# The last eight GRU cells: products gate by gate in three banks, another form of the new state, idle products behind a step's products

## The chip, the cores and the metric

The kernel runs as one program on one core of a Trainium2 chip. The metric is the device time of one launch in microseconds (us). Three runs of the kernel before took 2911.01, 2905.47 and 2907.79 us; the median is 2907.79 us. The profile and the trace are of one further execution, which took 2913.18 us; its first and last instruction are 2911.3 us apart.

The engines are named as the profile names them: PE multiplies matrices (PEld is its weight load), DVE, ACT and POOL are the vector, scalar and general engines, and SP issues the DMAs. All arithmetic is in float32.

## The reference, cut to what matters

Four layers follow each other, each added to the running x of shape 8 x 256 x 512: a masked attention, an attention with modulation, a network of 512 coupled oscillators that is stepped over the 256 columns with a fourth-order Runge-Kutta rule, and a GRU that is stepped over the same 256 columns. The change touches only the end of the last one:

```
def cell(h, x):
    gi = x @ W_ih + b_ih
    gh = h @ W_hh + b_hh
    i_r, i_z, i_n = jnp.split(gi, 3, axis=-1)
    h_r, h_z, h_n = jnp.split(gh, 3, axis=-1)
    r = jax.nn.sigmoid(i_r + h_r)
    z = jax.nn.sigmoid(i_z + h_z)
    n = jnp.tanh(i_n + r * h_n)
    h_new = (1.0 - z) * n + z * h
    return (h_new, h_new)
```

The batch is 8 and h has 512 features. GRU step tau needs the oscillators' output of step tau (its x) and the GRU's state of step tau - 1.

## The kernel before, in words

`scans` runs the oscillators and the GRU side by side. The loop variable t counts oscillator steps; the GRU runs `LAG` = 7 steps behind, at tau = t - 7. So the loop goes on for 8 more rounds, t = 256 to 263, in which `osc` is false and only the GRU works: the cells 248 to 255 and the products of the steps 249 to 255. These eight rounds are called the tail here. The order of the work is written out by hand (`tc.manual_schedule()`): each engine does its instructions in the order in which the loop emits them.

A GRU step has two parts. `gru_products(tau, s)` (L791) multiplies the state by the recurrent weights: 4 blocks k of the contraction times 3 gates times 4 output blocks j, 48 products in all, spread over the sub-steps s = 1, 2, 3 by `FILL` (8, 20 and 20 products). Each shows as two matmul instructions in the trace, so a step has 96. The three gates share one PSUM tile `pg_ps`: the state tile `hzs[tau % 3]` holds the state at three offsets among zeros, so that gate g of a block lands in rows 8g to 8g+7 of each group of 32 rows.

The cell comes in four pieces. `gru_1` (L808) transposes the whole tile (L810), adds the input part of all three gates at once (L812), takes the tanh for r (L817) and z (L819) on ACT, and forms z, z h and 1 - z on POOL (L821, L823, L825). `gru_2` forms n's argument on DVE (L829, L831) and its tanh on ACT (L832). `gru_3` multiplies n by 1 - z (L835). `gru_4` adds z h and writes the new state three times (L840, 96 columns), and POOL adds it to the output tile `x3T` (L847).

The rest of the tail: `input_gates(c, part)` (L771) multiplies x by the input weights for the next group of `TS` = 4 steps, at t = 256, 257 and 258, ahead of the step's recurrent products. `input_gate_out` (L782) transposes one gate of that (L784) and adds its bias on POOL (L786); there are three, two at t = 258 and one at t = 259. `write_out(c)` (L849) transposes 4 finished steps (L852) and issues 4 DMAs on SP (L854). `keep_warm(rounds)` (L859) issues products whose result nobody reads, 4 a round, into `idle_ps`. In the tail it runs at s = 3 of every round, between the products of s = 2 and those of s = 3 (L893), and at s = 0 where there is no input product (L891).

`ic_ps` are the two PSUM tiles of the oscillators' coupling products (L760, read by L952). Nothing uses them after t = 255.

Of the kernel before, what the change touches and what calls it, by code (L numbers as in the profile page):

```python
# [8 lines left out]
F32 = mybir.dt.float32  # L9
AF = mybir.ActivationFunctionType  # L10
ALU = mybir.AluOpType
# [3 lines left out]
P = 128  # L15
B, T, D = 8, 256, 512
# [574 lines left out]
def scans(ctx, tc, cst, bias, b_ih, b_hh, x2T, out):  # L591
# [51 lines left out]
    def rows(j):  # L643
        return slice(32 * j, 32 * j + 32)
# [156 lines left out]
                    )  # L801

    gru = {}

    def of_step(tau):
        return slice(B * (tau % TS), B * (tau % TS) + B)

    def gru_1(tau):  # L808

        nc.vector.transpose(pgt.rearrange("p m n -> p (m n)"), pg_ps)  # L810
        v = tmp.tile([P, 12, B], F32, tag="v", name=f"v_{tau}", bufs=2)
        nc.vector.tensor_add(  # L812
            v.rearrange("p (g m) b -> p g m b", m=NJ),
            pgt.rearrange("p m (g b) -> p g m b", b=B)[:, 0:3],
            gis[tau // TS % 3].rearrange("p (g m) n -> p g m n", m=NJ)[:, 0:3, :, of_step(tau)],
        )
        nc.scalar.activation(tr, v[:, 0:4, :], AF.Tanh, scale=0.5)  # L817
        tz = tmp.tile([P, NJ, B], F32, tag="tz", name=f"tz_{tau}", bufs=2)
        nc.scalar.activation(tz, v[:, 4:8, :], AF.Tanh, scale=0.5)  # L819
        z = tmp.tile([P, NJ, B], F32, tag="z", name=f"z_{tau}", bufs=2)  # L820
        nc.gpsimd.tensor_scalar(z, tz, 0.5, 0.5, ALU.mult, ALU.add)  # L821
        zh = tmp.tile([P, NJ, B], F32, tag="zh", name=f"zh_{tau}", bufs=2)
        nc.gpsimd.tensor_tensor(zh, z, hzs[tau % 3][:, :, 0:B], ALU.mult)  # L823
        z1 = tmp.tile([P, NJ, B], F32, tag="z1", name=f"z1_{tau}", bufs=2)
        nc.gpsimd.tensor_scalar(z1, tz, -0.5, 0.5, ALU.mult, ALU.add)  # L825
        gru.update(v=v, zh=zh, z1=z1)

    def gru_2(tau):
        stt(nn1, tr, 1.0, gru["v"][:, 8:12, :], ALU.add, ALU.mult)  # L829
        nn = tmp.tile([P, NJ, B], F32, tag="nn", name=f"nn_{tau}", bufs=2)  # L830
        stt(nn, nn1, 0.5, gis[tau // TS % 3][:, 12:16, of_step(tau)], ALU.mult, ALU.add)  # L831
        nc.scalar.activation(tn, nn, AF.Tanh)  # L832

    def gru_3():
        nc.vector.tensor_mul(hm, tn, gru["z1"])  # L835

    def gru_4(tau):

        hz = hzs[(tau + 1) % 3]
        nc.vector.tensor_tensor(  # L840
            state3(hz),
            hm.unsqueeze(2).to_broadcast([P, NJ, 3, B]),
            gru["zh"].unsqueeze(2).to_broadcast([P, NJ, 3, B]),
            ALU.add,
        )
        x = x3T[tau // TS][:, :, of_step(tau)]
        nc.gpsimd.tensor_tensor(x, x, hz[:, :, 0:B], ALU.add)  # L847

    def write_out(c):  # L849

        o = two.tile([P, NJ, 32], F32, tag="o", name=f"o_{c}")
        nc.vector.transpose(o.rearrange("p m n -> p (m n)"), x3T[c].rearrange("p m n -> p (m n)"))  # L852
        for j in range(NJ):
            nc.sync.dma_start(  # L854
                out[:, c * TS : (c + 1) * TS, j * P : (j + 1) * P].rearrange("b t n -> t b n"),
                o[rows(j)].rearrange("p m n -> p (m n)"),
            )

    def keep_warm(rounds):  # L859

        for k in range(rounds):
            for j in range(NJ):
                nc.tensor.matmul(
                    idle_ps[32 * j : 32 * j + B, :],
                    lhsT=condS[:, k, :],
                    rhs=cT_sb[:, k, j * P : (j + 1) * P],
                    start=True,
                    stop=True,
                )

    with tc.manual_schedule():
        made = []
        for t in range(T + LAG + 1):
            osc = t < T
            tau = t - LAG
            prod, cell = 0 <= tau < T, 1 <= tau <= T
            inp = TS <= t < T + TS
            c, part = t // TS - 1, t % TS
            if osc:
                if t % TS == 0:  # L880
                    x3T[t // TS] = chp.tile([P, NJ, 32], F32, tag="x3T", name=f"x3T_{t // TS}")
                qs = q
            for s in range(4):
                n = f"{t}_{s}"
                ic = ic_ps[s % 2]

                if osc:
                    coupling(tT, ic)
                if inp and s == 0:
                    input_gates(c, part)  # L890
                if t < T + LAG and (not prod or s == 0) and not (inp and s == 0 and INPUTS[part]):  # L891
                    keep_warm(2)
                if not osc and t < T + LAG and s == 3:  # L893
                    keep_warm(2)

                if osc:
                    sq, mm, hq = sqmm[:, 0, s % 2], sqmm[:, 1, s % 2], hqs[:, s % 2]
                    nc.scalar.activation(sq, qs, AF.Square, scale=math.sqrt(CUB[s]))  # L898
                if cell and s == 0:
                    gru_1(tau - 1)  # L900
                if cell and s == 1:
                    gru_2(tau - 1)

                if osc:
                    if s == 3:
                        stt(W[:, 4], qs, PQ[3], W[:, 4], ALU.mult, ALU.add)
                        p = st.tile([P, NJ, B], F32, tag="p", name=f"p_{t}")
                        nc.vector.tensor_scalar(p, W[:, 4], CLAMP - OFF, -CLAMP - OFF, ALU.min, ALU.max)  # L908
                    stt(mm, sq, LIN[s], qs, ALU.subtract, ALU.mult)  # L909
                if cell and s == 1:  # L910
                    gru_3()
                if osc:
                    nc.vector.tensor_sub(hq, W[:, s], mm)  # L913
                if cell and s == 1:
                    gru_4(tau - 1)
                if prod:
                    gru_products(tau, s)
                if osc:
                    if s < 3:
                        take(s, qs)  # L920
                    if s == 2 and t // US_CH + 1 < T // US_CH:
                        drive(t // US_CH + 1, t % US_CH // NJ, t % NJ)
                    if t == 0 and s < 3:

                        for i in range(*((0, 5), (5, 10), (10, 16))[s]):
                            drive(0, i // NJ, i % NJ)
                    if 0 < t < TS and s > 0:
                        gru_init(3 * t - 3 + s - 1)
                    if t == TS and s == 1:
                        gru_init(9)  # L930
                    if s == 3 and t + 1 < T:
                        W_next = linear_p(t + 1, p)

                if s == 3:

                    now, made = made, []
                    if cell and (tau - 1) % TS == TS - 1:
                        made.append((tau - 1) // TS)
                    if not osc:
                        now, made = now + made, []  # L940
                    for x in now:
                        write_out(x)
                if inp and (part, s) in ((2, 2), (2, 3), (3, 2)):
                    input_gate_out(c, {(2, 2): 0, (2, 3): 1, (3, 2): 2}[part, s])

                if osc:
                    qn = tmp.tile([P, NJ, B], F32, tag="qn", name=f"qn_{n}", bufs=4)
                    tTn = []
                    for half in range(2):
                        m2 = slice(half * HM, (half + 1) * HM)  # L950
                        icT = tmp.tile([P, HM, 32], F32, tag=f"icT{half}", name=f"icT{half}_{n}", bufs=2)
                        nc.vector.transpose(icT.rearrange("p m n -> p (m n)"), ic[:, half * 64 : half * 64 + 64])  # L952
                        stt(qn[:, m2, :], icT[:, :, 0:B], IC[s], hq[:, m2, :], ALU.mult, ALU.add)  # L953
                        if s < 3 or t + 1 < T:

                            tTn.append(tanh_half(qn, half, n))
                    tT = tTn
                    qs = qn
            if osc:
                q = st.tile([P, NJ, B], F32, tag="q", name=f"q_{t}")  # L960
                nc.gpsimd.tensor_scalar(q, qs, CLAMP, -CLAMP, ALU.min, ALU.max)
                if t + 1 < T:
                    W = W_next
                x = x3T[t // TS][:, :, of_step(t)]
                nc.gpsimd.tensor_tensor(x, x2T[:, :, :, t], q, ALU.add)  # L965
# [98 lines left out]
```

## Time and profile before

| what | us |
|---|---|
| median of three runs (lowest, highest) | 2907.79 (2905.47, 2911.01) |
| the profiled execution | 2913.18 |
| its span | 2911.3 |
| last oscillator transpose on DVE ends | 2857.6 |
| first product of GRU steps 249, 250, 251, 252 starts | 2860.51, 2866.25, 2871.99, 2877.72 |
| first product of GRU steps 253, 254, 255 starts | 2885.12, 2890.86, 2898.26 |
| last transpose of the output (L852) starts | 2905.99 |

The tail is thus some 53 us of the 2911.3 us. In it, one cell waits for one step's products and the next step's products wait for that cell. The table gives the start of each step's first product, so that the difference of two neighbours is a step. Before the tail the oscillators set the pace and the GRU's work lies between theirs.

### The profile page before, as it was taken

The page shows a single profiled execution, that of the slowest core. Times are in us where ns is not written, and L with a number is a line of the kernel's source. Part 1 is how long each engine was busy: PE and PEld are TensorE (multiplying, and loading weights), DVE is VectorE, ACT ScalarE, POOL GpSimd, SP SyncE. Part 2 cuts the span into 40 slices and gives each one's busy share as a digit, 9 for nine tenths or more (in the row PEclk, how much of TensorE's full clock was granted, in tenths as well). Part 3 has the DMA queues.
Part 4 walks back from the last instruction along what each step waited for, and adds up shares of the span by engine and source line. Part 5 has one row for each costly group of instructions (what it writes and reads, how often), then busy time and mean ns, then how long its engine had stood idle before and what let it go on. Part 6 is the DMA issues. An engine that isn't in the chain of part 4 may idle for free.

```text
span 2911.3 us, 159789 instructions
## 1 busy us (share of the span) xinstructions
PE 2711.6 (93%) x67258; PEld 1922.8 (66%) x67258; DVE 2127.1 (73%) x8951; ACT 1719.3 (59%) x8427; POOL 1096.2 (38%) x2945
## 2 busy tenths in 40 slices
PE   8799999999989999999999999999999999999996
PEld 3244444444557777777777777777777777777776
DVE  6767777775357777777777777777777777777773
ACT  5666566664346666666666666666666666666651
POOL 0134333443213444444444444444444444434442
PEclk7899999999999999999999999999999999999999
DMA  3111110101600000000000000000000000000000
GB/s 145 40 41 41 37 41 26 48 19 34 130 2 5 7 6 7 6 7 6 7 6 7 7 6 7 7 6 6 8 6 7 6 7 6 7 7 6 6 7 6
DMA packets 27559, 57.58 MB, mean 20 GB/s; under 512 B 2817, under 2 KB 17165, under 8 KB 24789
## 3 DMA queue, kind: packets, MB, share of 16 engines
q1 hardware_dynamic: 26836, 47.36, 5.3%
q8 instruction: 525, 8.60, 1.2%
q14 instruction: 198, 1.61, 0.2%
HBM read 40.15 MB, written 7.21 MB: 16 GB/s over the span
## 4 chain that ended last, share of the span: by engine, by line
PE 57%; DVE 28%; ACT 8%; issue 4%; POOL 1%; DMA 1%; ACTq 0%; SPq 0%; POOLq 0%; DVEq 0%
PE pg L795 20%; PE ic L760 18%; DVE icT L952 5%; DVE qn L953 5%; PE psqkv L321 5%; ACT tT L660 4%; DVE hqs L913 3%; PE pc L254 3%; DVE own L810 3%; DVE sqmm L909 2%; DVE v L812 2%; PE pc L167 2%; PE s L211 2%; DVE hz L840 2%; PE n L372 1%
## 5 line engine op out<-in xcount | busy, mean ns | idle before, releaser
L760 PE MATMUL ic<-cT_sb,tT 128*8 128x128 f32 x32736 | 1086.5, 273 | 81.3 <-ACT tT L660 44.5
L760 PEld LDWEIGHTS ic<-cT_sb,tT 128*8 128x8 f32 x32736 | 760.0, 89 | 338.5 <-ACT tT L660 267.9
L795 PE MATMUL pg<-whh_sb,hz 128*32 128x128 f32 x24576 | 821.2, 275 | 49.8 <-DVE hz L840 17.8
L660 ACT ACTIVATE tT<-qn 128x16 f32<-128x16 f32 x2046 | 441.0, 216 | 637.6 <-DVE qn L953 516.8
L795 PEld LDWEIGHTS pg<-whh_sb,hz 128*32 128x32 f32 x24576 | 670.3, 110 | 124.0 <-DVE hz L840 123.2
L952 DVE STREAM_TRANSPOSE icT<-ic 128x64 f32<-128x64 f32 x2048 | 504.6, 246 | 66.8 <-PE ic L760 62.2
L953 DVE SCALAR_TENSOR_TENSOR qn<-icT,hqs 128x16 f32<-128x16 f32 x2048 | 350.7, 171 | 70.1
L755 POOL TENSOR_TENSOR W<-W,cx 128x128 f32<-128x128 f32 x765 | 297.4, 389 | 256.3 <-ACT cx L741 256.2
L748 POOL TENSOR_TENSOR W<-cx,us 128x128 f32<-128x128 f32 x255 | 116.9, 458 | 444.5 <-ACT cx L741 444.5
L909 DVE SCALAR_TENSOR_TENSOR sqmm<-sqmm,qn 128x32 f32<-128x32 f32 x768 | 153.6, 200 | 151.9 <-ACT sqmm L898 122.7
L913 DVE TENSOR_TENSOR hqs<-W,sqmm 128x32 f32<-128x32 f32 x1020 | 200.1, 196 | 46.4 <-DVE own L835 1.3
L774 PE MATMUL gi<-wih_sb,x3T 128*32 128x384 f32 (+2 forms) x3072 | 201.5, 379 | 0.5 <-POOL x3T L965 0.5
L741 ACT ACTIVATE cx<-qn 128x32 f32<-128x32 f32 x1280 | 200.9, 213 | 0.0
L321 PE MATMUL psqkv<-wqkv_sb,xnT 128*128 128x512 f32 x384 | 174.6, 600 | 2.9 <-ACT sc L216 2.7
L221 DVE TENSOR_REDUCE mxp<-sc 128x4 f32<-128x2048 f32 x64 | 146.1, 2283 | 38.0 <-ACT sc L216 38.0
L741 ACT ACTIVATE cx<-p 128x32 f32<-128x32 f32 x1020 | 149.8, 217 | 32.1 <-DVE p L908 1.3
L216 ACT COPY sc<-s 128x512 f32<-128x512 f32 x256 | 131.8, 609 | 45.6 <-PE s L211 45.6
L239 DVE TENSOR_TENSOR sc<-sc,bc 128x2048 f32<-128x2048 f32 x64 | 148.5, 2321 | 9.6 <-DMA bc<-row 9.5
L810 DVE STREAM_TRANSPOSE own<-pg 128x128 f32<-128x128 f32 x256 | 84.8, 331 | 94.6 <-PE pg L795 94.6
L243 ACT ACTIVATE sc<-sc,negT 128x2048 f32<-128x2048 f32 x64 | 129.1, 2020 | 35.8 <-DVE sc L239 35.8
L741 ACT ACTIVATE cx<-q 128x32 f32<-128x32 f32 x1020 | 145.5, 213 | 0.0
L898 ACT ACTIVATE sqmm<-qn 128x32 f32<-128x32 f32 x768 | 140.5, 183 | 0.8
(149 smaller groups left out, 3360.4 us busy)
## 6 DMA issues: line engine op xcount, KB each, us to landing
bc<-row SPq DMA_DIRECT2D x16, 1024.0 KB
x<-in_x SPq DMA_DIRECT2D x8, 512.0 KB
out<-o SPq DMA_DIRECT2D x256, 16.0 KB
wqkv_sb<-in_L_cond_W_qkv SPq DMA_DIRECT2D x1, 3072.0 KB
wih_sb<-in_L_cond_W_ih SPq DMA_DIRECT2D x4, 768.0 KB
whh_sb<-in_L_cond_W_hh SPq DMA_DIRECT2D x4, 768.0 KB
x2d<-x2o SPq DMA_DIRECT2D x11, 256.0 KB
x2T<-x2d SPq DMA_DIRECT2D x11, 256.0 KB
```

What stands on the lines that cost most here:

```text
L321: nc.tensor.matmul(ps, lhsT=xnTs[b][:, c, m * P : (m + 1) * P], rhs=wqkv_sb[:, c, part * D : (part + 1) * D], start=(c == 0), stop=(c == N ...
L660: nc.scalar.activation(tT, src[:, half * HM : (half + 1) * HM, :], AF.Tanh)
L741: nc.scalar.activation(c[:, i], x, AF.Copy, scale=f)
L755: nc.gpsimd.tensor_tensor(W[:, i + 1 : 5], W[:, i + 1 : 5], c, ALU.add)
L760: nc.tensor.matmul(ps[32 * j : 32 * j + B, :], lhsT=tT[k // HM][:, k % HM, :], rhs=cT_sb[:, k, j * P : (j + 1) * P], start=(k == 0), stop= ...
L774: nc.tensor.matmul(gi_ps[rows(j), g0:g1, :], lhsT=x3T[c][:, k, :], rhs=wih_sb[:, k, g0:g1, j * P : (j + 1) * P], start=(k == 0), stop=(k = ...
L795: nc.tensor.matmul(pg_ps[rows(j), :], lhsT=hzs[tau % 3][:, k, 32 * g : 32 * g + 32], rhs=whh_sb[:, k, g, j * P : (j + 1) * P], start=((k, ...
L810: nc.vector.transpose(pgt.rearrange("p m n -> p (m n)"), pg_ps)
L909: stt(mm, sq, LIN[s], qs, ALU.subtract, ALU.mult)
L913: nc.vector.tensor_sub(hq, W[:, s], mm)
L952: nc.vector.transpose(icT.rearrange("p m n -> p (m n)"), ic[:, half * 64 : half * 64 + 64])
L953: stt(qn[:, m2, :], icT[:, :, 0:B], IC[s], hq[:, m2, :], ALU.mult, ALU.add)
```

## The change

For t < 256 the emitted order is as before. For t >= 256 the loop body is a branch of its own. Cell 248 still uses `gru_1` to `gru_4`; the cells 249 to 255 use `tail_cell`, and the products of the steps 249 to 255 come from `tail_products`.

`tail_products` runs the gates one after the other in the order r, n, z (g = 0, 2, 1), each over all four blocks k, each into a PSUM tile of its own: `pg_ps` and the two `ic_ps`. `tail_sum` transposes one gate and adds its input part. `tail_cell` does r, then n, then z, and forms the new state as n + z (h - n): with tz = tanh(z's argument / 2), that is 0.5 (tz + 1) (h - n) + n, on DVE. The new state is written once, not three times.

In a round the cell now comes first, then (at t = 259) all three `input_gate_out`, the step's products, the input products, the idle products (2 rounds behind input products, else 6, none in the last two rounds) and the output.

```
+    gate_ps = (pg_ps, *ic_ps)
...
+    def tail_products(tau):
+        for g in (0, 2, 1):
+            for k in range(NJ):
+                for j in range(NJ):
+                    nc.tensor.matmul(
+                        gate_ps[g][rows(j), :],
+                        lhsT=hzs[tau % 3][:, k, 0:32],
+                        rhs=whh_sb[:, k, g, j * P : (j + 1) * P],
+                        start=(k == 0),
+                        stop=(k == NJ - 1),
+                    )
+
+    def tail_sum(tau, g):
+        x = tmp.tile([P, NJ, 32], F32, tag="tg", name=f"tg_{tau}_{g}", bufs=2)
+        nc.vector.transpose(x.rearrange("p m n -> p (m n)"), gate_ps[g])
+        v = tmp.tile([P, NJ, B], F32, tag="tv", name=f"tv_{tau}_{g}", bufs=4)
+        gi = gis[tau // TS % 3][:, 4 * g : 4 * g + 4, of_step(tau)]
+        nc.vector.tensor_add(v, x[:, :, 0:B], gi)
+        return v
+
+    def tail_cell(tau):
+
+        h, hz = hzs[tau % 3][:, :, 0:B], hzs[(tau + 1) % 3]
+        vr = tail_sum(tau, 0)
+        nc.scalar.activation(tr, vr, AF.Tanh, scale=0.5)
+        vn = tail_sum(tau, 2)
+        stt(nn1, tr, 1.0, vn, ALU.add, ALU.mult)
+        nn = tmp.tile([P, NJ, B], F32, tag="nn", name=f"nn_{tau}", bufs=2)
+        stt(nn, nn1, 0.5, gis[tau // TS % 3][:, 12:16, of_step(tau)], ALU.mult, ALU.add)
+        nc.scalar.activation(tn, nn, AF.Tanh)
+        vz = tail_sum(tau, 1)
+        tz = tmp.tile([P, NJ, B], F32, tag="tz", name=f"tz_{tau}", bufs=2)
+        nc.scalar.activation(tz, vz, AF.Tanh, scale=0.5)
+        d = tmp.tile([P, NJ, B], F32, tag="zh", name=f"d_{tau}", bufs=2)
+        nc.vector.tensor_sub(d, h, tn)
+        e = tmp.tile([P, NJ, B], F32, tag="z", name=f"e_{tau}", bufs=2)
+        stt(e, tz, 1.0, d, ALU.add, ALU.mult)
+        stt(hz[:, :, 0:B], e, 0.5, tn, ALU.mult, ALU.add)
+        x = x3T[tau // TS][:, :, of_step(tau)]
+        nc.gpsimd.tensor_tensor(x, x, hz[:, :, 0:B], ALU.add)
...
-                    lhsT=condS[:, k, :],
-                    rhs=cT_sb[:, k, j * P : (j + 1) * P],
+                    lhsT=condS[:, k % NJ, :],
+                    rhs=cT_sb[:, k % NJ, j * P : (j + 1) * P],
...
+            if not osc:
+                if cell and tau - 1 >= T - LAG:
+                    tail_cell(tau - 1)
+                elif cell:
+                    gru_1(tau - 1)
+                    gru_2(tau - 1)
+                    gru_3()
+                    gru_4(tau - 1)
+                if inp and part == 3:
+                    for g in range(3):
+                        input_gate_out(c, g)
+                if prod:
+                    tail_products(tau)
+                if inp:
+                    input_gates(c, part)
+                if prod and t + 1 < T + LAG:
+                    keep_warm(2 if inp and INPUTS[part] else 6)
+                if cell and (tau - 1) % TS == TS - 1:
+                    made.append((tau - 1) // TS)
+                for x in made:
+                    write_out(x)
+                made = []
+                continue
...
-                    keep_warm(2)
-                if not osc and t < T + LAG and s == 3:
                     keep_warm(2)
...
-                    if not osc:
-                        now, made = now + made, []
```

## The prediction

> **What bounds the kernel now.** Nothing before the last oscillator step is edited, so I looked for the stretch that can move. The page first: PE is busy 93% of the span, but that is an average over three layers and says nothing of a tail of 53 us. Then the chain of waits in the tail, GRU step 253 from its first product to that of step 254 (columns: start, length, what; "x56" counts matmul instructions):
>
> ```profile
> 2885.12 1.74 PE pg L795 x56
> 2886.86 0.44 PE idle L863 x16
> 2887.30 1.14 PE pg L795 x40
> ...
> 2888.46 0.34 DVE own L810
> ...
> 2888.82 0.27 DVE v L812
> ...
> 2889.25 0.22 ACT tz L819
> ...
> 2889.55 0.23 POOL z L821
> ...
> 2889.85 0.25 POOL zh L823
> 2890.10 0.19 POOL z L825
> ...
> 2890.32 0.21 DVE own L835
> ...
> 2890.55 0.27 DVE hz L840
> ...
> 2890.86 2.63 PE pg L795 x56
> ```
>
> The reader is to see a ring with no slack: products 3.34 us (2885.12 to 2888.46), then the cell 2.40 us (to 2890.86), 5.74 us together. Sixteen idle instructions stand inside the products and cost 0.44. The cell's bound is z's way over POOL, not n's.
>
> Some steps are longer: 7.40 us for 252 and 254, and step 255 too. The table of stretches says why (length, then busy time of PE, PEld, DVE, ACT and POOL, then the granted clock); I cut it every 3.41 us, the spacing on which the slow stretches fall:
>
> ```profile
> 2864.10:2867.51 3.41, 1.80 (x60) 1.32 (x56) 1.18 (x6) 0.55 (x3) 0.90 (x4) 1.00 0.02 5
> ...
> 2887.99:2891.40 3.41, 1.37 (x52) 1.08 (x47) 1.44 (x6) 0.55 (x3) 0.90 (x4) 1.00 0.04 7
> 2891.40:2894.81 3.41, 3.41 (x76) 3.25 (x72) 0.00 (x0) 0.00 (x0) 0.00 (x0) 0.52 0.00 0
> 2894.81:2898.23 3.42, 1.42 (x48) 1.13 (x40) 1.44 (x6) 0.55 (x3) 0.65 (x3) 0.98 0.02 5
> 2898.23:2901.64 3.41, 3.38 (x65) 3.27 (x69) 0.00 (x0) 0.00 (x0) 0.25 (x1) 0.52 0.00 0
> ```
>
> A stretch in which PE was busy 1.37 or 1.42 us is followed by one at clock 0.52; after 1.80 it is not. There are three such cold stretches (the first at 2877.75), each adding 7.40 - 5.74 = 1.66 us.
>
> **The change, part by part.**
>
> *Products.* A step keeps its 96 instructions. The idle ones leave the middle: -0.44. Pace: 40 instructions take 1.09 us from start to start (2887.01 to 2888.10 on the weight load), 27.3 ns each; 112 of them then make 3.06, and DVE started at 3.34, so 0.28 is the pipeline and the release. Counted from the step's first product, r's 32 are readable at 0.87 + 0.28 = 1.15, n's at 2.03, z's at 2.90.
>
> Can DVE read one bank while PE fills another? The timeline of the last oscillator step shows it:
>
> ```profile
> 2856.77 1.28 PE L795 MATMUL pg<-whh_sb,hz 128*32 128x128 f32 x40
> 2857.02 0.25 DVE L952 STREAM_TRANSPOSE icT<-ic 128x64 f32<-128x64 f32 x1 [0.26 <-PE ic L760]
> 2857.30 0.17 DVE L953 SCALAR_TENSOR_TENSOR qn<-icT,hqs 128x16 f32<-128x16 f32 x1
> 2857.39 0.24 DVE L952 STREAM_TRANSPOSE icT<-ic 128x64 f32<-128x64 f32 x1
> ```
>
> The transpose of `ic` starts under the products into `pg`. And the second transpose, which needs nothing of L953, starts 0.09 after it, while L953, which needs its transpose, started 0.28 after that one: independent DVE instructions overlap.
>
> *The cell.* Durations: a 128x128 transpose from PSUM to SBUF 0.30 (L784 in the tail), next dependent start 0.33; a 128x32 add or three-operand instruction 0.19 to 0.20 (L829, L831, L835), next start 0.23; tanh to its DVE reader 0.23 (2889.11 to 2889.34). r: transpose 1.15, add 1.48, tanh 1.71, usable 1.94. n: transpose 2.03, add 2.36, L829's kind 2.59, L831's kind 2.82, tanh 3.05, usable 3.28. z: ready at 2.90, but DVE is in order, so behind 2.82 by some 0.1: transpose 2.93, add 3.26, tanh 3.49, usable 3.72. h - n goes beside z's tanh (3.38 to 3.58). Then e 3.72, the new state 3.95, and PE starts 0.25 later (L840's 0.31 with 258 ns; 96 columns become 32, 200 ns): **4.20 us a step**. So 1.54 less than 5.74: 0.44 of idle products and 1.10 of the cell (2.40 to 1.30 behind the last product). If DVE lets nothing overlap, z starts at 3.05 and the step is 4.32; I take 4.20, since the row above shows overlap, and keep 4.32 for the range.
>
> Here a rule speaks against the change. The Trainium skill, "VectorE: DVE Perf Modes", section on the TRN2 errata, says that latency is paid per instruction, so that many small tiles cost more than one large. DVE goes from 6 to 11 instructions a cell, and with all of them in the ring a step is 5.75 (worked out under the second rival). The rows put r's and n's six under the products, with only z's behind them: 4.20. I take the rows.
>
> *Idle products and clock.* They now stand behind the products: 48 instructions (6 rounds), 1.31 us, so PE has issued everything at 2.62 + 1.31 = 3.93, before the state is there at 4.20: no cost, 0.27 of slack. PE is then busy over 90% of a step, and cold stretches should go. Behind input products it is 0.87 + 0.44 of the same.
>
> One gap opens instead. Before, the input products of t = 256 ran while cell 248 was computed (16 instructions, 1.07 us). Now step 249's products stand ahead of them, so PE waits from 2858.05 (last product of 248) to 2860.51 (state there): 2.46 us. The Trainium skill, "TensorE: Matmul & The Clock Gate", section "Why this matters for your kernels", says that gaps above about 3 us between bursts throttle. By that, 2.46 is free, but so were the 2.04 us gaps that went cold here. By the rows it is a stretch from 2857.27 to 2860.68 with about 1 us busy, below the 1.42 that went cold: 3.41 us at half clock, +1.66. I take the row. The 3.41 us grid is not tied to the kernel: on a random phase a gap g goes cold if about 1.8 of it falls into one stretch, 67% for 2.46 (28% with no boundary inside, 39% with one near an end), 54% for 2.04.
>
> *Moved work.* At t = 259 three gate transposes and the one of `write_out` follow cell 251 on DVE, ahead of step 252's r. The third waits for a buffer (two of them) until POOL has added the first gate (0.25 for `x3T`, then 0.46 each): DVE is free at about 1.35, r's transpose slips by 0.20, and r's tanh has 2.59 - 1.94 = 0.65 to spare: nothing. Without that cover it is 0.2 once. The four DMAs of that chunk go to an SP queue that has nothing else; POOL loses three instructions a cell; its last addition of gates ends near 1.6, before or just at the add that might ask for it (1.48).
>
> *The end.* For cell 255 the state comes at 3.95, POOL's addition 4.23, L852 4.52. What follows (5.3 us to the end of the span) stays.
>
> **Sum.** Before, 2860.51 to 2905.99 is 45.48. After: 6 x 4.20 + 4.52 = 29.72, less by 15.8: 10.8 of work and 5.0 of three cold stretches. With +1.66 for the new gap it is -14.1: the profiled execution's 2913.18 would be 2899.1. The median of the runs is 5.4 lower; some of that can be fewer cold stretches. With four gaps of 2.04 at 54%, a run has 2.2 of them, 3.6 us. So against the median: 10.8 + 3.6 - 0.67 x 1.66 = 13.3, and **2894.5**.
>
> **The rivals.**
>
> *The clock stays as it was* (11%): idle products behind the last real one don't hold it, and three cold stretches stay beside the new gap's. 2907.79 - 10.8 + (3 - 2.2) x 1.66 + 1.1 = 2899.4. For: idle products inside the step did not prevent 1.4 of 3.41. Against: those covered 0.6 us of a gap of 2 to 2.7, the new ones nearly all.
>
> *It doesn't do what it says* (8%, and 2% for other ways to no change): DVE gets r's bank only when all products are done, or r's release comes late. Then DVE's instructions stand in line from 2.90: r's transpose 2.90 and add 3.23, n's transpose 3.46, add 3.79, L829's kind 4.02, L831's kind 4.25, z's transpose 4.48, add 4.81, tanh 5.04, e 5.27, state 5.50, PE 5.75. The tail is 6 x 5.75 + 6.07 = 40.6, plus 1.1 for the new gap, against 44.2 (45.48 with 2.2 cold stretches in place of 3): 2905.3, no change. The `ic` row speaks against it.
>
> *Slower* (5%): the idle products become the bound. PE takes its instructions in order, so the next step's products wait for 48 idle ones. At half clock these take 2.62, far above the slack; a step is then 144 x 54.6 ns = 7.86, the last 5.24 + 1.90 = 7.14, the tail 54.3 against 44.2: 2917.9. It decides from about four of seven steps cold ((44.2 - 29.7) / 3.66). Against: the fully busy stretches in the table are followed by clock 0.98 or 1.00, so a cold stretch should heal after 3.41 us.
>
> **The numbers.** 74% for the forecast, 11, 8 + 2 and 5% for the others. About 0.2% (5.8 us) is what a measurement here can tell from no change. Faster: 74 + 11 = 85%; same 10%; slower 5%. Range: low, all cold stretches gone and none new, from a median that had three (10.8 + 5.0 = 15.8, 2892.0), less 3 for the scatter of three runs (5.5 wide); high, the first rival's 2899.4 with 0.8 for DVE without overlap and 1.3 of scatter. So 2889 to 2901.5.
>
> **What would show it.** Right: first products of the steps 250 to 255 come 4.2 us apart; r's and n's transposes start under the products; e and the state follow z's tanh, POOL is out of the ring; clock 0.5 once at most, at the start of the tail. Wrong: r's transpose starts behind z's last product; PE starts a step at the end of its idle products and not on the state; clock 0.5 in later steps; or the stretch before 2857 differs, where no edit reaches.

## The result and the profile after

Six runs of the changed kernel took 2889.26 to 2902.27 us, median 2894.74; the kernel before, with three further runs, has a median of 2908.74. The ratio is 0.9954, with a 95% interval of 0.9941 to 0.9967: 9.6 to 17.2 us less. The forecast was 2894.5.

The profiled execution of the changed kernel is the fastest of the six: 2889.26 us, span 2887.5, so 23.8 us less than the span before. Not all of that is the change. Step 249's first product starts at 2851.02 in place of 2860.51, so 9.5 us of it lie ahead of the tail, where nothing was edited. The view of one line's instructions (count, shortest, median and longest ns, first and last start) shows where, by the oscillators' first tanh; before, then after:

```profile
L660 ACT ACTIVATE tT<-qn x2046: 197/216/221, 837.6 to 2856.0; 128x16 f32<-128x16 f32 x186
```

```profile
L660 ACT ACTIVATE tT<-qn x2046: 199/216/218, 828.1 to 2846.5; 128x16 f32<-128x16 f32 x186
```

The 9.5 us are there at the first of the 2046 instructions and unchanged at the last: they arise ahead of it, where the two attention layers are. The traces' records of the clock go with that. Ahead of this tanh they show half clock for 85.3 us before and for 61.4 us after; over the fourteen profiles it is 61 to 79 us in the eight whose oscillators start by 833.6 us, and 82 to 92 us in the six where they start at 837.4 or later. Why one execution has more of it than another was not tested.

So I read every kernel below on its tail, from the first product of step 249 to the start of the last output transpose. One profile gives that to some 0.1 us where no stretch is at half clock, since the same step repeats to 0.02 us from profile to profile. The table of stretches for the tail (length, busy time of PE, PEld, DVE, ACT, POOL with the number of instructions, granted clock; the last two columns, on DMA, are not used here), before and after:

```profile
2860.51:2905.99 45.48, 31.32 (x880) 28.13 (x880) 11.20 (x48) 3.85 (x21) 7.83 (x32) 0.89 0.02 5
```

```profile
2851.02:2882.18 31.16, 27.62 (x912) 24.47 (x912) 17.13 (x83) 4.42 (x21) 3.30 (x11) 1.00 0.03 8
```

45.48 became 31.16, and the clock 0.89 became 1.00: 14.3 us, of which 5.0 are the three cold stretches and 9.3 is work that left the ring. The 5.3 us behind the last transpose are the same. DVE's busy time went up, from 11.20 us in 48 instructions to 17.13 in 83, as the objection in the prediction had it, but most of that lies under the products. The chain of waits for one step of the changed kernel (an instruction is listed from where it takes over, so one that overlaps its predecessor starts later here than in a timeline):

```profile
2868.68 1.08 PE pg L856 x32
2869.77 0.92 PE ic L856 x32
...
2870.71 0.33 DVE tg L866
...
2871.06 0.20 DVE tv L869
...
2871.36 0.21 DVE own L878
...
2871.59 0.19 DVE nn L880
2871.78 0.23 DVE tg L866
...
2872.04 0.19 DVE tv L869
2872.23 0.11 DVE d L886
2872.34 0.23 ACT tz L884
...
2872.59 0.20 DVE e L888
...
2872.81 0.20 DVE hz L889
...
2873.06 1.08 PE pg L856 x32
```

The step is 4.38 us (2868.68 to 2873.06); 5.74 before. PE is in the chain for r's and n's products only: from 2870.71 on DVE carries it, with z's tanh on ACT near the end, and z's products run beside n's transpose and sums. POOL is gone from it. r's transpose is not in the chain; the timeline has it under n's products, which start at 2869.77:

```profile
2869.83 0.32 DVE L866 STREAM_TRANSPOSE tg<-pg 128x128 f32<-128x128 f32 x1 [1.20 <-PE pg L856]
```

### The profile page after: what moved, and what is told of

It reads as the page before. It is cut to its first block, busy times and chain, and to the rows that moved or that the text cites. A ratio compares the mean times of both kernels' runs of the same rounds, so it can differ in the third digit from the quotient of the medians.

```text
span 2887.5 us, 159836 instructions
## 1 busy us (share of the span) xinstructions
PE 2693.6 (93%) x67274; PEld 1910.3 (66%) x67274; DVE 2132.2 (74%) x8986; ACT 1719.6 (60%) x8427; POOL 1091.7 (38%) x2924
## 4 chain that ended last, share of the span: by engine, by line
PE 56%; DVE 29%; ACT 8%; issue 4%; POOL 1%; DMA 1%; ACTq 0%; SPq 0%; POOLq 0%; DVEq 0%
PE pg L795 19%; PE ic L760 18%; DVE icT L1015 5%; PE psqkv L321 5%; DVE qn L1016 5%; ACT tT L660 4%; DVE hqs L978 3%; DVE own L811 3%; PE pc L254 3%; DVE sqmm L974 2%; DVE v L813 2%; PE pc L167 2%; DVE hz L841 2%; PE s L211 2%; PE n L372 1%
## 5 line engine op out<-in xcount | busy, mean ns | idle before, releaser
L795 PE MATMUL pg<-whh_sb,hz 128*32 128x128 f32 x23904 | 795.4, 274 | 37.4 <-DVE hz L841 5.6
L795 PEld LDWEIGHTS pg<-whh_sb,hz 128*32 128x32 f32 x23904 | 648.0, 110 | 108.5 <-DVE hz L841 108.3
L380 DVE TENSOR_REDUCE mxp<-n 128x2 f32<-128x512 f32 x128 | 79.5, 684 | 77.5 <-PE n L372 77.5
```

Of the source, the lines that this page charges most:

```text
L795: nc.tensor.matmul(pg_ps[rows(j), :], lhsT=hzs[tau % 3][:, k, 32 * g : 32 * g + 32], rhs=whh_sb[:, k, g, j * P : (j + 1) * P], start=((k, ...
```

## The experiments

Each kernel is told by its difference from the changed one. "Warm" means without a stretch at half clock.

**Which part brings it.** Idle products moved, with products and cell of before (`e5`: `tail_products` calls the old `gru_products`, and the old cell always runs):

```
-        for g in (0, 2, 1):
...
+        for s in range(1, 4):
+            gru_products(tau, s)
...
-                if cell and tau - 1 >= T - LAG:
+                if False:
```

> Products and cell of before in the order of the changed kernel: only the idle and input products move behind the step's products. Theory: 2.90 for the products and 2.40 for the cell, 5.30 a step, 37.4 us for the tail, and no cold stretch behind the first gap. Rival (the clock stays as it was): 5.30 a step with two or three cold stretches, 40.7 to 42.4.

Measured: 5.30 to 5.37 us a step, the first 6.97 with one cold stretch, tail 39.16: 37.5 warm. The theory's 5.30 holds, and no later gap went cold.

Gate by gate, with z over POOL (`e3`):

```
-        nc.vector.tensor_sub(d, h, tn)
...
-        stt(e, tz, 1.0, d, ALU.add, ALU.mult)
-        stt(hz[:, :, 0:B], e, 0.5, tn, ALU.mult, ALU.add)
...
+        nc.gpsimd.tensor_scalar(z, tz, 0.5, 0.5, ALU.mult, ALU.add)
...
+        nc.gpsimd.tensor_tensor(zh, z, h, ALU.mult)
...
+        nc.gpsimd.tensor_scalar(z1, tz, -0.5, 0.5, ALU.mult, ALU.add)
+        nc.vector.tensor_mul(hm, tn, z1)
+        nc.vector.tensor_tensor(hz[:, :, 0:B], hm, zh, ALU.add)
```

> The changed kernel with z's share in the form of before (z, z h and 1 - z on POOL, then n (1 - z) and the sum on DVE). Theory (the two parts only pay together): z's transpose starts at 3.02 us of the step, its tanh at 3.64, POOL 3.94 to 4.7, the state at 4.94, so 5.19 a step and a tail of 36.7 us without cold stretches. Rival (each part brings its own half of the gain): about 34.3.

Measured: 5.22 us a step (5.64 where the three input gates are read out), tail 37.28, no cold stretch. Its chain, from z's tanh to the next step:

```profile
2885.36 0.24 ACT tz L884
...
2885.68 0.23 POOL z L886
...
2885.97 0.25 POOL zh L888
2886.23 0.19 POOL z L890
...
2886.44 0.21 DVE own L891
...
2886.68 0.20 DVE hz L892
```

Once r and n are out of the way, z's three POOL instructions stand in the ring: 0.84 us from z's tanh ending (2885.60) to DVE's first (2886.44). The long step is not the read-outs' own time: 0.35 of its 0.42 us stand ahead of L878, which starts 0.65 us behind its add in place of 0.30, with no wait for another engine in the trace. `e3b` and `e7` have the same 0.35 in the same step. Its cause is not known; the other 0.07 is told below.

The form n + z (h - n), with one bank and one add for all gates (`e4`; half of h comes from POOL off the ring, `hh`, so that the last sum can write the state three times):

```
+        hh = tmp.tile([P, NJ, B], F32, tag="z1", name=f"hh_{tau}", bufs=2)
+        nc.gpsimd.tensor_scalar(hh, h, 0.5, 0.0, ALU.mult, ALU.add)
...
-        nc.vector.tensor_sub(d, h, tn)
+        stt(d, tn, -0.5, hh, ALU.mult, ALU.add)
```

> The changed kernel with the products of before (one bank, all gates of a block together, one transpose and one add for all gates), but the state as n + z (h - n) on DVE (half of h comes from POOL, off the ring, and the state is written three times, as before). Theory (the two parts only pay together): all of r's and n's chain stands behind the last product: transpose 2.90, add 3.26, tanh 3.55, 3.78, 4.02, tanh 4.24, difference 4.47, 4.70, state 4.93, PE 5.24, so 5.24 a step and a tail of 37.0 us without cold stretches. Rival (each part brings its own half): about 34.3.

Measured: 5.31 us a step (5.45 once), the first 6.97 with one cold stretch, tail 39.28: 37.6 warm. Its chain:

```profile
2886.14 0.34 DVE own L869
...
2886.50 0.27 DVE v L871
...
2886.80 0.21 ACT own L876
...
2887.03 0.21 DVE own L879
...
2887.26 0.20 DVE nn L881
...
2887.49 0.21 ACT own L882
```

Here z's tanh is not in the ring at all, but r's and n's whole chain stands behind the last product. Together:

| | warm tail, us |
|---|---|
| before | 40.5 |
| idle products moved (e5) | 37.5 |
| moved, and gate by gate (e3) | 37.3 |
| moved, and n + z (h - n) (e4) | 37.6 |
| all three (the change) | 31.2 |

By the step it is 5.30 us with the moved idle products, 5.22 and 5.31 with one part more, and 4.38 with both. So gate by gate alone is worth 0.08 us a step, the other form alone nothing, and both together 0.92, which is the tail's 6.3. (The 37.3 has the 0.35 us in it that is not understood.) There are two chains behind the products, r to n and z over POOL, of nearly one length. Shortening one leaves the other. The order of the gates and the three banks came together; neither was run without the other.

**Do the idle products hold the clock?** `e1` has none in the tail:

```
-                if prod and t + 1 < T + LAG:
-                    keep_warm(2 if inp and INPUTS[part] else 6)
```

> The changed kernel without any idle products in the tail. Measured on the tail: from the first product of step 249 to the start of the last output transpose, 45.48 us before (40.5 without its three cold stretches) and 31.16 after. Theory (a gap of PE goes cold when about 1.8 us of it falls into one 3.41 us stretch): behind z's last product PE now waits only some 1.6 us of a 4.38 us step, so no step goes cold but perhaps the first, and the tail stays at 31.2 (32.8 with the first). Rival (the idle products are what holds the clock): two or three more cold stretches, 34.5 to 36.

Measured: 5.95 for the first step, then 4.36 to 4.44, tail 32.68. One cold stretch, the first gap's. Its table of stretches, cut at the edges of the cold one:

```profile
2853.33:2856.74 3.41, 0.94 (x36) 0.67 (x30) 2.04 (x10) 0.55 (x3) 1.36 (x6) 1.00 0.02 5
2856.74:2860.15 3.41, 3.41 (x72) 3.40 (x68) 0.81 (x3) 0.20 (x1) 0.02 (x1) 0.50 0.06 17
...
2873.81:2877.22 3.41, 1.80 (x68) 1.60 (x64) 1.70 (x9) 0.43 (x2) 0.25 (x1) 1.00 0.07 18
```

Without idle products PE is busy 1.80 us in the emptiest of the later stretches, and it stays warm. At 4.38 us a step they are not needed. They are at 5.22: the gates-alone kernel without them (`e3b`, the same two lines removed).

> The gates-alone kernel (z's share over POOL, 5.22 us a step) without idle products. Theory: PE now waits 2.4 us a step, and where more than about 1.8 us of that falls into one stretch of the 3.41 us grid the next stretch is cold: three to five cold stretches, tail 41.7 to 45 (37.3 with the idle products). Rival (a step's real products hold the clock, and the idle ones were never needed): 37.3.

Measured: 5.22 a step up to step 253 (5.65 for step 252, as in `e3`), 6.75 for step 254, and 7.11 from the first product of step 255 to the end of the tail (5.53 in `e3`); tail 40.39, with two cold stretches in place of none. I had expected three to five, because I forgot that three of the gaps still hold 0.87 us of input products. The stretches:

```profile
2874.30:2877.71 3.41, 1.55 (x56) 1.55 (x60) 0.94 (x5) 0.23 (x1) 0.91 (x4) 1.00 0.04 10
2877.71:2881.13 3.42, 1.28 (x48) 1.01 (x40) 1.66 (x8) 0.63 (x3) 0.65 (x3) 1.00 0.02 5
2881.13:2884.54 3.41, 3.15 (x60) 2.93 (x64) 0.70 (x3) 0.20 (x1) 0.25 (x1) 0.50 0.00 0
```

Busy 1.55 us is followed by a warm stretch, 1.28 by a cold one. The kernel before narrows it. The prediction's 1.42 stood on an edge that is 0.13 us too early, as the clock of 0.98 in its row shows. On the edges at which the records change the clock, all three stretches ahead of a cold one have 1.37 or 1.38; one of them, and a later one that is followed by a warm stretch:

```profile
2894.94:2898.35 3.41, 1.37 (x52) 1.08 (x46) 1.44 (x6) 0.55 (x3) 0.71 (x4) 1.00 0.02 5
2901.76:2905.18 3.42, 1.44 (x52) 1.17 (x44) 1.04 (x5) 0.55 (x3) 0.65 (x3) 1.00 0.00 0
```

With 1.43 (`e3`) and 1.45 (`e7` below), both warm, the limit is about 1.4 us of 3.41, so 2.0 idle, and not the 1.8 that I used. It is a limit for this part of the program. In the attention layers, kernel before, a stretch that is listed as fully busy has half clock behind it:

```profile
48.22:51.63 3.41, 3.41 (x27) 2.66 (x26) 1.84 (x6) 1.27 (x3) 0.21 (x1) 1.00 0.00 0
51.63:55.05 3.42, 3.42 (x17) 1.08 (x16) 3.42 (x2) 2.54 (x5) 0.00 (x0) 0.50 0.01 2
```

So the busy time of a profile is not all that the clock goes by; what else counts was not tested.

**The first gap.** The changed kernel itself had none of its 2.46 us gap cold. The grid explains it; cut on the edges that its earlier cold stretches give:

```profile
2846.23:2849.65 3.42, 2.32 (x88) 1.94 (x76) 2.34 (x12) 0.77 (x5) 0.47 (x2) 1.00 0.02 5
2849.65:2853.06 3.41, 2.04 (x76) 2.04 (x80) 1.46 (x8) 0.40 (x2) 0.90 (x4) 1.00 0.02 5
```

An edge at 2849.65 splits the gap, 1.1 and 1.4 us, and both stretches stay above the limit. I ran the changed kernel again, with five timed runs, next to a kernel that puts the first input products back ahead of step 249's products (`e6`):

```
+                if t == T:
+                    input_gates(c, part)
                 if prod:
                     tail_products(tau)
-                if inp:
+                if inp and t > T:
                     input_gates(c, part)
                 if prod and t + 1 < T + LAG:
-                    keep_warm(2 if inp and INPUTS[part] else 6)
+                    keep_warm(2 if t > T and inp and INPUTS[part] else 6)
```

> The changed kernel again, on the same chip as the one with the gap filled. Theory: 13.3 us less than the kernel before in the median (forecast), of which the tail's 45.48 to 31.2 or 32.8 is 12.7 to 14.3; the start of step 249, which lies behind code that is not edited, falls anywhere between 2850 and 2861 us, as in the profiles so far. Rival (the move of the program's earlier part belongs to the change): step 249 always starts before 2857 here, and the gain is over 18 us.

> The changed kernel with the first input products (t = 256) put back ahead of step 249's products, and 6 rounds of idle products behind these. Theory: PE then works 1.07 us of the 2.46 us before step 249, as it did in the kernel before, no stretch is idle for 1.8 us, and the first step takes 4.4 us on any phase of the grid: tail 31.2 in every run, where the changed kernel has 31.2 or 32.8. Against the kernel before 14 to 15.5 us faster in the median. Rival (the first gap does not matter, or the input products delay step 249): tail of 32 to 33.

Measured: the changed kernel again 2896.85 us (2893.37 to 2899.43), ratio 0.9953 (0.9941 to 0.9964). Its first gap fell into one stretch this time, but for 0.2 us of it, as the two rows show, and the tail was 32.67:

```profile
2850.67:2854.08 3.41, 1.12 (x44) 0.90 (x32) 2.05 (x10) 0.55 (x3) 1.14 (x5) 1.00 0.02 5
2854.08:2857.50 3.42, 3.22 (x64) 2.98 (x68) 0.88 (x4) 0.20 (x1) 0.25 (x1) 0.50 0.05 14
```

With the gap filled the tail is 31.11, although there too the gap lay wholly inside one stretch, which now has PE busy for 2.01 us, and the next one stays at full clock:

```profile
2859.75:2863.16 3.41, 2.01 (x52) 1.17 (x48) 2.17 (x10) 0.55 (x3) 1.24 (x6) 1.00 0.02 5
```

In ten profiles the gap is open. In five it lay in one stretch and the next went cold (`e0`, `e1`, `e4`, `e5`, and `e8` below); in the other five an edge split it and none did (the changed kernel, `e3`, `e3b`, `e2` and `e7`). The medians don't show it: 2899.31 (2893.23 to 2902.59), ratio 0.9957 (0.9943 to 0.9970), so 11.3 us less than the kernel before where 14 to 15.5 was expected. A saving of 1.66 in some runs is below the scatter of the unedited part: over all fourteen profiles step 249 starts between 2851.0 and 2863.0 us, and in `e6` it was 2862.96. The rival of `e0_changed` is out: the changed kernel gains 13.7 us in that set, not over 18, and though its own step 249 starts early again (2854.28), kernels with the same order ahead of the tail start it as late as 2862.96.

**Can idle products become the bound?** More of them (`e2`):

```
-                    keep_warm(2 if inp and INPUTS[part] else 6)
+                    keep_warm(8 if inp and INPUTS[part] else 12)
```

> The changed kernel with 12 rounds of idle products in place of 6, and 8 in place of 2 behind input products. Theory (PE takes its instructions in order, so idle products beyond the slack delay the step): 192 instructions of 27.3 ns issue in 5.24 us, so 5.24 a step in place of 4.38 and a tail of 36.2 us (37.8 with a cold first step). Rival (idle products never hold up real ones): 31.2.

Measured: 5.23 to 5.26 us a step, tail 36.34. PE's list of waits over the whole tail has one entry, the gap before step 249:

```profile
PE pg L856 <- DVE hz L841: 2.4, 1, 2.4
```

The state is always there first; the step's length is the number of instructions in PE's queue. That is the mechanism of the slower rival, at full clock. Its price at half clock was not run, and nothing in the changed kernel brings it about.

**Why 4.38 and not 4.20.** In the changed kernel the product with n's sum (L878) starts 0.30 us after the add in front of it, where I had taken 0.23; it waits for ACT (tr) and for DVE's own add. `e8` forms tr + 1 by an instruction of its own, earlier:

```
+        tr1 = tmp.tile([P, NJ, B], F32, tag="v", name=f"tr1_{tau}", bufs=2)
+        nc.vector.tensor_scalar_add(tr1, tr, 1.0)
         vn = tail_sum(tau, 2)
-        stt(nn1, tr, 1.0, vn, ALU.add, ALU.mult)
+        nc.vector.tensor_mul(nn1, tr1, vn)
```

> The changed kernel with tr + 1 formed by a DVE instruction of its own ahead of n's transpose, so that the product with n's sum waits for DVE alone. In the changed kernel that product starts 0.29 to 0.30 us after the add in front of it, with a semaphore instruction of DVE's queue in between, where I had taken 0.23. Theory (a wait for two engines costs a semaphore instruction and some 0.06 us): the product starts 0.23 after its add, and the step is 4.32 to 4.36 us in place of 4.38. Rival (no cost of the second wait): 4.38 or, with one instruction more on DVE, above.

The timeline of the changed kernel, then of `e8`:

```profile
2871.06 0.19 DVE L869 TENSOR_TENSOR tv<-tg,gis 128x32 f32<-128x32 f32 x1
...
2871.36 0.20 DVE L878 SCALAR_TENSOR_TENSOR own<-own,tv 128x32 f32<-128x32 f32 x1
```

```profile
2876.52 0.19 DVE L869 TENSOR_TENSOR tv<-tg,gis 128x32 f32<-128x32 f32 x1
2876.75 0.20 DVE L880 TENSOR_TENSOR own<-tr,tv 128x32 f32<-128x32 f32 x1
```

0.30 became 0.23. L878 also became a plain product, but the kind is not the cause: L880, which kept it, starts 0.23 behind L878 in the changed kernel, with one wait. So the second wait costs 0.07. The step takes 4.33 to 4.40 in place of 4.37 to 4.44, so it gains 0.04 only: the added instruction holds up n's transpose, and n's add starts 2.41 behind the step's first product in place of 2.37.

The same price shows without an edit. In step 252 of the changed kernel, L880 waits for POOL too (the input gates), has a semaphore instruction ahead of it, and starts 0.31 behind L878; in the other six steps it has none and starts 0.23 behind, as in the chain above:

```profile
2866.91 0.20 DVE L878 SCALAR_TENSOR_TENSOR own<-own,tv 128x32 f32<-128x32 f32 x1
2867.22 0.19 DVE L880 SCALAR_TENSOR_TENSOR nn<-own,gis 128x32 f32<-128x32 f32 x1
```

The last sum, L889, has such an instruction in the steps 251 and 255 and starts 0.30 behind L888 there, 0.23 in the other five.

z's tanh is late too: 0.28 to 0.30 after its add, against 0.23 for r's. `e7` takes h - n off DVE, because z's tanh starts just when that ends:

```
-        nc.vector.tensor_sub(d, h, tn)
+        nc.gpsimd.tensor_tensor(d, h, tns, ALU.subtract)
```

> The changed kernel with h - n on POOL (n's tanh goes to SBUF for that). In the changed kernel z's tanh starts 0.28 to 0.30 us after the add in front of it, where r's starts 0.23 after its own, and just when h - n ends on DVE. Theory (the following DVE instruction holds up the add's release to ACT): without it z's tanh starts 0.23 after its add and the step is 4.31 to 4.35 us in place of 4.38. Rival (the delay has another cause): 0.28 and 4.38, or more if the POOL result comes late.

Measured: still 0.28, and 4.44 us a step, because POOL's result comes late (one step 4.86). The theory falls: h - n is not the cause. The next theory was a second wait on ACT, since z's tanh has a semaphore instruction on ACT's queue ahead of it in every step. `e9` puts its result into the shared tile `own`, together with three other edits (tr + 1 early, the first gap filled, no idle products):

```
-        tz = tmp.tile([P, NJ, B], F32, tag="tz", name=f"tz_{tau}", bufs=2)
+        tz = hm
```

> The changed kernel with tr + 1 formed early, z's tanh written to the bank tile `own` in place of a rotating tile, the first input products ahead of step 249's products, and no idle products in the tail. Theory: z's tanh lost 0.05 to 0.07 us to a second wait (its trace shows a semaphore instruction on ACT's queue, which r's and n's tanh do not have) and 0.03 to its target in SBUF; the idle products are not needed at a step of 4.3 us; and the first gap stays above the clock's threshold. So z's tanh starts 0.23 after its add, a step takes 4.24 to 4.30 us, no stretch goes cold on any phase, and the tail takes 30.2 to 30.6. Against the kernel before 14.5 to 16 us faster in the median, within a scatter of 5. Rival (the late tanh has another cause): 4.34 a step and 30.9. Rival (without idle products the clock drops): 32.5 or more.

Measured: 4.52 to 4.59 a step, tail 32.19, no cold stretch; 2898.79 us in the median, ratio 0.9972 (0.9960 to 0.9985), so 8.5 us less than the kernel before where 14.5 to 16 was expected. The edit made a new wait:

```profile
2889.30 0.20 ACT L886 ACTIVATE own<-tv 128x32 f32<-128x32 f32 x1 [0.31 <-DVE tv L869]
2889.53 0.19 DVE L888 TENSOR_TENSOR d<-hz,own 128x32 f32<-128x32 f32 x1 [0.33 <-ACT own L886]
```

h - n reads n from `own`, so it now waits for z's tanh, which writes there. In the changed kernel it ran beside it. And the tanh is still 0.28 late: the semaphore instruction is still ahead of it in all seven steps, so the edit did not remove what it was meant to. `e7` has the comparison, in n's tanh (L882). There it has a semaphore instruction in six of seven steps, and none in step 252; a step with one, and step 252:

```profile
L882 ACTq EVENT_SEMAPHORE  x6: 17/17/17, 2854.9 to 2882.0; - x6
...
2859.12 0.19 DVE L880 SCALAR_TENSOR_TENSOR nn<-own,gis 128x32 f32<-128x32 f32 x1
2859.40 0.23 ACT L882 ACTIVATE tns<-nn 128x32 f32<-128x32 f32 x1 [1.26 <-DVE nn L880]
...
2868.43 0.19 DVE L880 SCALAR_TENSOR_TENSOR nn<-own,gis 128x32 f32<-128x32 f32 x1
2868.65 0.23 ACT L882 ACTIVATE tns<-nn 128x32 f32<-128x32 f32 x1 [1.62 <-DVE nn L880]
```

0.28 with it, 0.22 without, as for r's tanh, which never has one. So a second wait costs 0.06 on ACT too, and this accounts for z's tanh; no run took it away from that one. With `tz` back in its own tile (`e10`, the other three edits kept):

> The last one with z's tanh back in its own rotating tile: the changed kernel with tr + 1 formed early, the first input products ahead of step 249's products, and no idle products in the tail. Theory: h - n no longer waits for z's tanh (the shared tile made it, 4.53 us a step), so 4.34 a step as with tr + 1 early alone, no cold stretch, and a tail of 30.7 to 30.9 us, the shortest of all. In the median it can't be told from the changed kernel (0.3 to 1.9 us less, within a scatter of 5). Rival (another dependence): 4.5 a step.

Measured: 4.33 to 4.41 a step, tail 30.89, no cold stretch; 2893.45 us (2892.05 to 2898.99), ratio 0.9941 (0.9923 to 0.9958). By its tail it is the shortest, 0.3 us less than the changed kernel's lucky phase and 1.8 less than the other; in the median the two can't be told apart. Its step 249 started late as well, at 2861.03.

## Why the prediction was right, point by point

- *Products.* r was to be readable at 1.15, n at 2.03, and DVE's transposes start 1.15 and 2.03 behind the step's first product (2869.83 and 2870.71 behind 2868.68). The pace of 27.3 ns and the release of 0.28 hold, and DVE reads one bank while PE fills the next. The rival in which the release comes late is out.
- *The cell.* The structure is as worked out. The size is off: 4.38 in place of 4.20, a tail of 31.16 in place of 29.72. The terms that were mis-sized: L878's wait for two engines (0.30 for 0.23), z's tanh behind its add (0.28 to 0.30 for 0.23), its own length into SBUF (0.23 for 0.20), and the transposes' next start (0.35 for 0.33, twice). In the step shown these are 0.07, 0.05, 0.04 and 0.03, and 0.01 came back elsewhere: the missing 0.18. The first two are second waits, which the prediction put at nothing.
- *Idle products and clock.* No cold stretch behind the first step: right, but for another reason than given. The shorter step alone does it (`e1`); the idle products do nothing at 4.38 us. Where the gap is 2.4 us they do matter (`e3b`).
- *The first gap.* It goes cold or not by the phase of the 3.41 us grid, and costs 1.56 to 1.67 us against 1.66 forecast; five of ten open gaps, against 67%. The limit of 1.8 us idle was too low; with 2.0 the same sum gives 55%, but ten gaps can't tell the two apart.
- *Moved work.* r's transpose of step 252 slipped by 0.03, not 0.20, and cost nothing, as forecast. The steps 251 and 252 take 4.44 in place of 4.38 all the same, where I had nothing: each has one second wait for POOL, in L889 and L880.
- *The sum.* 10.8 us of work was forecast, 9.3 measured; the three cold stretches' 5.0 went in the profile; the median moved by 14.0 against 13.3. With 9.3 the forecast's own sum gives 11.8, which the interval holds as well. The shortfall of the cell was hidden by the scatter of the part that nobody edited, whose twelve us over the profiles are as large as the gain. That 2894.5 and 2894.74 lie so close is luck.

## What to carry to other kernels

Where two chains of nearly one length stand behind the same event, shorten both or neither: each half of this change alone was worth 0.1 us a step or less, and both together 0.9. A serial loop's gain is read on the loop, step by step, in one profile; whole-program times here scatter by as much as the gain. Before adding work to keep a clock up, work out how much of a stretch the engine is busy without it. Where an instruction starts 0.06 or 0.07 us later than its like, look for a semaphore instruction ahead of it.

## What the runs showed of the hardware

- The clock changes on a grid of 3.41 us that is not tied to the program: in all fourteen traces its changes lie a whole number of such stretches apart, and the grid falls differently on the same step. From the start of the oscillators on, every stretch at full clock with PE listed busy for at most 1.38 us was followed by one at half clock, none with 1.43 us or more was. The pauses in the tail that did this were 2.0 to 2.5 us long, and the same pause did nothing when an edge split it. The Trainium skill's figure of about 3 us ("TensorE: Matmul & The Clock Gate", section "Why this matters for your kernels") is too long for them, and the measurement decides. Ahead of the oscillators the limit does not hold: of 177 stretches at full clock there that were followed by one at half clock, over the fourteen traces, 125 had PE listed busy for 1.43 us or more.
- A second wait puts a semaphore instruction ahead of an instruction. With it, a DVE instruction started 0.30 us behind the DVE instruction that it needs (L878, L880, L889), 0.23 without; a tanh of 128x32 on ACT (gate by gate) 0.28 to 0.31 behind the DVE instruction that it needs, 0.22 to 0.23 without.
- A DVE instruction more is not free because DVE has idle time elsewhere: in `e8` it stood ahead of n's transpose and took back 0.03 of the 0.07 us that it saved.
